# Attention with a gated mixture of experts on one core: where the second batch's sums are made, and the bank of a pair's sixth product

## The chip, the cores and the metric

The kernel runs on one core of a Trainium2 chip. The metric is the device time of one launch in microseconds. The runs shown are three; the profile is one further execution, with its own time.

## The reference

`x` has 2 batches of 2048 tokens of 512 features. Everything is float32. Cut to what matters:

```python
x = L0_attn_x
xn = layernorm(x)
# attention on xn
x_norm = layernorm(xn) * gamma + beta
q, k, v = x_norm @ qkv                     # 512 -> 3 x 512
scores = q @ k.T / sqrt(512)               # causal, per batch
out = softmax(scores) @ v
s = out @ o_proj + xn
# experts on xn: 8 experts, 2 chosen for a token, hidden 352
top_scores, top_idx = top_k(xn @ gate_w.T + gate_b + bias, 2)
comb = one_hot(top_idx) weighted by softmax(top_scores)
h = silu(xn @ w1 + b1)
y = (h @ w2 + b2) summed with comb
return x + s * silu(y)
```

## The kernel before

The kernel has three stages, and all of its work is put in an order written out by hand: every engine runs its instructions in the order in which the program emits them, so an instruction that waits holds back all that comes after it on the same engine, and the same is true of each engine's DMA queue. There is no planner.

1. Up to about 200 us: normalization, folding of weights, projections to queries, keys and values (stored in DRAM), and routing.
2. Up to about 610 us: the experts, 68 slots of 128 tokens, with results in `y_d` in DRAM.
3. From there: attention, with the gate and the output. The change lies here.

Attention works on tiles of 128 queries. There are 32 tiles, `NT`, and the loop `for s in range(NT + OUT + 2)` (L1409) takes one per step. The list `seq` (L810) says which: steps 0 to 15 are the tiles 15 to 0 of the first batch, and steps 16 to 31 are tiles 8, 9, 0, 1, 6, 7, 2, 3, 4, 5, 10, 11, 12, 13, 14, 15 of the second. Keys and values come in blocks of 512 tokens, `NBB` = 4 to a batch. `K` is 4, the first block of the second batch.

A step `s` emits, in this order:

- every second step, the loads of the next pair's queries (`fetch_q`, on the SP queue);
- `attended` (L1348) for a tile three or four steps back: ACT scales and shifts the product with values, DVE adds the residual; and `emit`, which is on POOL (multiply by the gate, add `x`) and stores the output;
- the scores of tile `s` on PE, in chunks of up to 512 keys (`chunk_scores`, L989), each in a PSUM bank of pool `ps_a`; DVE masks the diagonal and takes maxima. Between the chunks DVE runs `join_p` (L1168), which puts together the probabilities of tile `s-1` that a DMA has transposed;
- `end_scores` (L1080: the negated maximum `nm`), `divisor` (L1312), `exponentials` (L1131): ACT writes the probabilities, POOL splits them into 16-bit halves (`pu`), an SP DMA transposes them (`puT`). A tile of up to 384 keys is turned by PE instead (`turn_p`, L1161: transposes into a bank of `ps_a`, and a copy on ACT);
- up to four loads of the second batch's keys and values (`fetch_parts`, SP queue; the list `parts_b` gives the step from which each is due), and some sums on DVE, of which below;
- the product with values of tile `s-2` (`values`, L1175; a bank of `ps_b`), or the pieces of the fast form;
- every second step `gate` (L1338): four DVE operations on two rows of the experts' results, then a Silu on ACT; and `gather_y`, POOL's indirect loads of such rows.

The pairs in `FAST` (L959), which are steps 0 to 7 and 26 to 31, take a fast form with seven products in place of eight. `fast_scores` (L1029) does it for scores against the first two blocks, `values_first`, `values_next` and `values_end` (L1257 to L1310) for the product with values. These need sums made ahead on DVE:

- `query_sums` (L1007, tile `sq`, one buffer): four operations on the pair's queries, made in the odd step before;
- `block_sums` (L1018, tile `tk`, one buffer): four operations on two blocks of keys, once for each batch;
- `combine_v` (L1201, tile `vT`, three buffers): four operations on one block of values; each of the fast form's three blocks has its own.

In `fast_scores` each of the seven products (`made`) takes a bank from the list `pools` in turn, and DVE adds the products to the scores in SBUF. The first one is copied out by ACT (L1065). The sixth is the one with `q[:, 3]` and `b22` (in the profile `p<-k,sq`), the seventh the one with `a22` and `k[:, 3]` (`p<-tk,q`, in its second appearance). `ps_a` has five banks, `ps_b` three (L1092 and L1093).

Before, the second batch's sums are placed by these lines at the end of the step's work on scores:

```python
combine = {20: K, 22: K + 1, 26: K + 2}
...
            if s in combine:
                combine_v(combine[s])
            if 21 <= s < 25:
                block_sums(K, (s - 20,))
            if s % 2 and s > 3 and s // 2 + 1 in FAST:
                query_sums(s + 1, nc.vector)
```

Of the kernel before, what the change touches and what calls it, by code (L numbers as in the profile page):

```python
# [26 lines left out]
def gated_attention_moe(  # L27
# [27 lines left out]
    nc = tc.nc  # L55
# [7 lines left out]
    NBB = S // TB  # L63
# [895 lines left out]
    FAST = (0, 1, 2, 3, 13, 14, 15)  # L959
# [5 lines left out]
    def begin_scores(s):  # L965
        b, t, first = place(s)
        widths[s] = [TB] * (b - first) + [(t + 1) * P]
        mx = sm.tile([P, NBB], F32, name=f"mx_{s}", tag="mx")
        nm = sm.tile([P, 1], F32, name=f"nm_{s}", tag="nm")
        scored[s] = mx, nm, []  # L970
# [36 lines left out]
    def query_sums(s, engine):  # L1007

        q = qsums[s] = sq.tile([P, 4, ND // 2, P], F32, name=f"sq_{s}", tag="sq")
        (a11, a12), (a21, a22) = (  # L1010
            [aqs[seq[s] // 2][:, d, ts(seq[s + i] % 2, P)] for d in kds] for i in range(2)
        )
        engine.tensor_tensor(q[:, 0], a21, a22, ALU.add)
        engine.tensor_tensor(q[:, 1], q[:, 0], a11, ALU.subtract)
        engine.tensor_tensor(q[:, 2], a11, a21, ALU.subtract)
        engine.tensor_tensor(q[:, 3], a12, q[:, 1], ALU.subtract)

    def block_sums(first, parts=(1, 2, 3, 4)):  # L1018

        if 1 in parts:  # L1020
            bsums[first] = kt.tile([P, 4, ND // 2, TB], F32, name=f"tk_{first}", tag="tk")
        k = bsums[first]
        (b11, b12), (b21, b22) = ([aks[first + j][:, d, :] for j in range(2)] for d in kds)
        for i, x1, x2 in (1, b12, b11), (2, b22, k[:, 0]), (3, b22, b12), (4, b21, k[:, 1]):
            if i in parts:
                engine = nc.gpsimd if i == 3 and first == 0 else nc.vector
                engine.tensor_tensor(k[:, i - 1], x1, x2, ALU.subtract)
# [64 lines left out]
    ps_b = psum(att, name="ps_b", bufs=3)  # L1092
    ps_a = psum(att, name="ps_a", bufs=5)  # L1093
# [13 lines left out]
    for i in range(NS):  # L1107
        experts_step(i)
        if i >= 8 and i % 2 == 0 and early:
            f, b, c = early.pop(0)  # L1110
# [90 lines left out]
    def combine_v(b, parts=(1, 2, 3, 4), engine=nc.vector):  # L1201

        v = avs[b].rearrange("p (i h) d -> p i h d", h=2)
        if b not in avts:
            avts[b] = cp.tile([P, 2, 4, D // 2], F32, name=f"vT_{b}", tag="vT", bufs=NBB - 1)
        t1, t2, t3, t4 = (avts[b][:, :, i, :] for i in range(4))
        b11, b12, b21, b22 = (v[:, :, h, c] for h in range(2) for c in (LO, HI))
        for i, dst, x1, x2 in (1, t1, b12, b11), (2, t2, b22, t1), (3, t3, b22, b12), (4, t4, b21, t2):
            if i in parts:
                engine.tensor_tensor(dst, x1, x2, ALU.subtract)  # L1210
# [115 lines left out]
    def gather_y(s):  # L1326

        rows[s] = [op.tile([P, 2, D], F32, name=f"yg0_{s}", tag="yg0")]
        for i in range(2):
            rows[s].append(op.tile([P, D], F32, name=f"yg1_{s + i}", tag="yg1"))  # L1330
            n = seq[s + i]
            for k, y in enumerate((rows[s][0][:, i, :], rows[s][-1])):
                nc.gpsimd.indirect_dma_start(  # L1333
                    out=y, out_offset=None, in_=y_d,
                    in_offset=bass.IndirectOffsetOnAxis(ap=posi[k][:, n : n + 1], axis=0),
                )
# [57 lines left out]
    K = NBB  # L1394
# [3 lines left out]
    parts_b = [(s, f, b, c) for s, f, b in parts_b for c in range(ND)]  # L1398
    parts_b.sort(key=lambda part: part[0])

    combine = {20: K, 22: K + 1, 26: K + 2}

    def fetch_parts(s, most):
        while parts_b and most and parts_b[0][0] <= s:
# [4 lines left out]
    for s in range(NT + OUT + 2):  # L1409
        fast = s // 2 - 1 in FAST  # L1410
        pair = (s, s + 1) if s // 2 in FAST else (s,)
        if s < NT and (s % 2 == 0 or len(pair) == 1):
            for k in pair:
                if s:
                    begin_scores(k)
                room(k)
        n = s // 2 + 1
        if s % 2 == 0 and NQ <= n < NT // 2:
            for c in range(2):
                fetch_q(n, c)  # L1420
        if s == 0:
            fetch_parts(s, NBB * ND)
            block_sums(0)
        late = []
        for k in range(NT):
            if k not in AHEAD:
                wait = 4 - k % 2 if k // 2 in FAST else 3
                if s == k + wait:
                    late.append((attended, k))
                if s == k + wait + 1:  # L1430
                    emit(k)
        if len(pair) == 1 or s % 2:
            for f, *args in late:
                f(*args)
        for k in range(NT):
            if s == (NT - 1 if k in AHEAD else k + 2 - k % 2 if k // 2 in FAST else k + 1):
                fetch_inputs(k)
        if s == NT - 1:
            gather_y(NT - 2)
        joins = []  # L1440
        for k in () if s == 1 else (0, 1) if s == 2 else (s - 1,):
            if 0 <= k < NT - 1 and not by_te(k):
                joins += [(join_p, k)] * len(halves[k])
        chunks = []
        if s < NT and s != 1:
            chunks = [(k, j) for k in ((1,) if s == 0 else (s,)) for j in direct(k)]
        if s == 0:

            for k, j in chunks:
                chunk_scores(k, j)  # L1450
            chunks = []
        if s < NT and s % 2 == 0 and len(pair) == 2:
            pools = [(ps_b, "b")] * (NBB - 1) + [(ps_a, "a")] if s < 3 else [(ps_a, "a")]
            if s == 2:
                joins = [(combine_v, b, (1,)) for b in range(NBB - 1)] + joins
            now = 5 if s == 2 else 1
            fast_scores(s, pools, late + joins[:now])
            joins = joins[now:]
            if s == 0:
                query_sums(2, nc.gpsimd)  # L1460
        for k, j in chunks:
            chunk_scores(k, j)
            if s != 3 and joins:
                f, *args = joins.pop(0)
                f(*args)
        if s != 3:
            for f, *args in joins:
                f(*args)
        if 0 <= s - 1 < NT and by_te(s - 1):

            values(s - 2)
            turn_p(s - 1)
        if s < NT and s != 1:
            end_scores(s)
        if fast and s % 2 == 0 and 2 < s < NT:
            combine_p(s - 2)
        if 0 <= s - 1 < NT:
            divisor(s - 1)
        if s < NT:
            if s != 1:  # L1480
                exponentials(s)
            if s % 2 == 0 and len(pair) == 2:
                maximum(s + 1, turned[s + 1][:, : 2 * TB], 0)
            if s == 0:
                end_scores(1)
                exponentials(1)
            fetch_parts(s, 4)
            if s in combine:
                combine_v(combine[s])
            if 21 <= s < 25:  # L1490

                block_sums(K, (s - 20,))
            if s % 2 and s > 3 and s // 2 + 1 in FAST:
                query_sums(s + 1, nc.vector)
        if s == 2:
            pass
        elif s == 3:
            combine_p(0, (1, 3, 2))
            for b in range(NBB - 1):
                combine_v(b, (2,))  # L1500
            values_first(0)
            combine_p(0, (4,))
            for b in range(NBB - 1):
                combine_v(b, (4,))
            values_next(0)
            for f, *args in joins:
                f(*args)
            values_end(0, [lambda: query_sums(s + 1, nc.vector)])
        elif fast and s % 2 == 0:
            values_first(s - 2)  # L1510

            if s != NT - 2:
                values_next(s - 2)
        elif fast and s == NT - 1:
            values_next(s - 3)
            gate(s - 1)
            values_end(
                s - 3, [lambda: join_p(s)] * len(halves[s]) + [lambda: combine_p(s - 1)]
            )
            for k in AHEAD:  # L1520
                make_ahead(k)
        elif fast:
            values_end(s - 3)
        elif 0 <= s - 2 < NT and not (s - 1 < NT and by_te(s - 1)):
            values(s - 2)

        for k in range(0, NT - 2, 2):
            if s == (k + 2 if k + 2 in AHEAD else k + 3):
                gate(k)
        for k in range(0, NT - 2, 2):  # L1530
            if s == k + 1:
                gather_y(k)
        if s == 1:
            for b in range(NBB - 1):
                combine_v(b, (3,), nc.gpsimd)
# [45 lines left out]
```

## Time and profile before

| | |
|---|---|
| median of 3 runs | 1059.25 us |
| lowest, highest | 1057.97, 1065.2 us |
| profiled execution | 1057.82 us |
| its span | 1056.1 us |
| PE busy | 1038.8 us (98%) |
| DVE busy | 644.1 us (61%) |
| POOL busy | 432.4 us (41%) |
| ACT busy | 312.6 us (30%) |

The span runs from the first to the last instruction; the rest of the execution's time lies around it. PE is TensorE, PEld its weight loads, DVE VectorE, ACT ScalarE, POOL GpSimd, SP the engine that issues most DMAs. A float32 matmul shows as two entries of PE, so a product over two chunks of 128 is "x4". The end of a matmul is modelled and overlaps the next start, so distances are better taken from start to start. In a line of the timeline, the brackets hold the time for which the engine was idle just before and the engine and line that ended it. Steps 10 to 13 of attention lie at 773 to 812 us of this profile, steps 20 to 27 at some 858 to 941 us (by PE's scores).

### The profile page before, as it was taken

The page shows a single profiled execution, that of the slowest core. Times are in us where ns is not written, and L with a number is a line of the kernel's source. Part 1 is how long each engine was busy: PE and PEld are TensorE (multiplying, and loading weights), DVE is VectorE, ACT ScalarE, POOL GpSimd, SP SyncE. Part 2 cuts the span into 40 slices and gives each one's busy share as a digit, 9 for nine tenths or more (in the row PEclk, how much of TensorE's full clock was granted, in tenths as well). Part 3 has the DMA queues.
Part 4 walks back from the last instruction along what each step waited for, and adds up shares of the span by engine and source line. Part 5 has one row for each costly group of instructions (what it writes and reads, how often), then busy time and mean ns, then how long its engine had stood idle before and what let it go on. Part 6 is the DMA issues. An engine that isn't in the chain of part 4 may idle for free.

```text
span 1056.1 us, 12196 instructions
## 1 busy us (share of the span) xinstructions
PE 1038.8 (98%) x3554; PEld 616.2 (58%) x3554; DVE 644.1 (61%) x1227; ACT 312.6 (30%) x643; POOL 432.4 (41%) x469
## 2 busy tenths in 40 slices
PE   8999999999999999999999999999999999899998
PEld 3687886444555555555545446676665544447577
DVE  4797884775333333334335459767655668688686
ACT  3222221211322322322355322122334443422330
POOL 2364250003433333334332127354547776754372
PEclk9999999999999999999999999999999999999999
DMA  8699989946999999999897257445668768744361
GB/s 302 180 283 282 282 263 339 340 142 171 221 221 227 222 233 228 223 232 218 207 187 159 58 191 180 118 101 139 184 169 270 214 202 231 185 112 120 96 156 40
DMA packets 300512, 209.33 MB, mean 198 GB/s; under 512 B 234520, under 2 KB 247576, under 8 KB 299424
## 3 DMA queue, kind: packets, MB, share of 16 engines
q1 hardware_dynamic: 281248, 146.12, 55.5%
q0 software_dynamic: 10560, 35.17, 13.0%
q10 hardware_dynamic: 8640, 27.27, 7.1%
q8 instruction: 30, 0.49, 0.2%
q14 instruction: 34, 0.28, 0.1%
HBM read 92.89 MB, written 60.03 MB: 145 GB/s over the span
## 4 chain that ended last, share of the span: by engine, by line
PE 77%; POOL 6%; issue 6%; DVE 5%; DMA 3%; ACT 2%; SPq 0%; ACTq 0%; POOLq 0%; DVEq 0%
PE py L921 16%; PE ph L882 15%; PE p L1236 9%; PE ps L994 8%; PE p L400 7%; PE p L1046 6%; PE pj L341 3%; PE pw L207 3%; PE po L1188 3%; PE pj L346 3%; PE p L1188 2%; POOL yg L1333 2%; POOL pu L1148 1%; DMA zuT<-zu 1%; POOL o L1362 1%
## 5 line engine op out<-in xcount | busy, mean ns | idle before, releaser
L921 PE MATMUL py<-w,ht 128*128 (+3 forms) x408 | 187.1, 594 | 0.0
L882 PE MATMUL ph<-w,xT 128*128 (+1 forms) x544 | 173.2, 460 | 0.7 <-POOL keep L1103 0.7
L929 DVE COPY y<-py 128x512 f32<-128x512 f32 x68 | 46.9, 690 | 179.0 <-PE py L921 172.9
L994 PE MATMUL ps<-k,q 128*128 128x512 f32 (+3 forms) x416 | 143.0, 495 | 0.0
L882 PEld LDWEIGHTS ph<-w,xT 128*128 128x128 f32 (+1 forms) x544 | 97.5, 181 | 73.1 <-issue 34.5
L907 ACT ACTIVATE ht<-ht,b1sel 128x128 f32<-128x128 f32 (+3 forms) x237 | 73.1, 375 | 224.1 <-DVE ht L901 224.1
L892 POOL COPY hu<-h 128x704 uint16<-128x704 uint16 x68 | 52.4, 771 | 204.1 <-ACT h L890 124.7
L1148 POOL COPY pu<-pT 128x1024 uint16<-128x1024 uint16 (+2 forms) x74 | 84.0, 1167 | 126.3 <-ACT pT L1138 67.3
L921 PEld LDWEIGHTS py<-w,ht 128*128 128x128 f32 (+3 forms) x408 | 73.4, 182 | 75.4 <-issue 37.4
L994 PEld LDWEIGHTS ps<-k,q 128*128 128x128 f32 x416 | 74.6, 190 | 67.6 <-issue 57.7
L768 POOL DMA_INDIRECT xs<-zu_d,toki x68 | 68.9, 1014 | 69.3 <-DVE toki L642 57.9
L1188 PE MATMUL po<-v,pT 128*128 128x512 f32 x182 | 81.2, 593 | 1.2 <-DVE pT L1170 1.2
L1333 POOL DMA_INDIRECT yg<-y_d,posi x64 | 64.2, 1003 | 36.5 <-DVE yg L1344 22.1
L264 POOL COPY zu<-z 128x1024 uint16<-128x1024 uint16 x32 | 35.2, 1100 | 78.0 <-DVE z L249 78.0
L1170 DVE COPY pT<-puT 128x1024 uint16<-128x1024 uint16 (+2 forms) x74 | 55.9, 787 | 7.4 <-DMA puT<-pu 7.4
L1188 PEld LDWEIGHTS po<-v,pT 128*128 128x128 f32 x182 | 34.0, 190 | 40.0 <-issue 37.8
L413 DVE TENSOR_TENSOR so<-p,so 128x512 f32<-128x512 f32 x70 | 45.8, 686 | 16.5 <-DMA v_d<-so 9.3
L1354 DVE SCALAR_TENSOR_TENSOR o<-xo,xscale,o 128x512 f32<-128x512 f32 x30 | 28.7, 962 | 41.9 <-ACT o L1351 17.3
L842 DVE COPY xT<-xhT 128x1024 uint16<-128x1024 uint16 x68 | 47.2, 693 | 10.6 <-PE ph L882 5.7
L1052 DVE TENSOR_TENSOR pT<-p,pT 128x512 f32<-128x512 f32 x49 | 32.8, 687 | 25.5 <-PE p L1046 13.8
L1362 POOL TENSOR_TENSOR o<-o,yg 128x512 f32<-128x512 f32 x30 | 41.8, 1393 | 13.5 <-DVE o L1354 12.5
L1138 ACT ACTIVATE pT<-ps,nm 128x512 f32<-128x512 f32 (+3 forms) x52 | 30.0, 581 | 56.6 <-DVE nm L1082 37.3
(246 smaller groups left out, 1670.5 us busy)
## 6 DMA issues: line engine op xcount, KB each, us to landing
y_d<-y SPq DMA_DIRECT2D x68, 256.0 KB
zu_d<-zu SPq DMA_DIRECT2D x32, 264.0 KB
x<-in_x_dram SPq DMA_DIRECT2D x32, 256.0 KB
kt_d<-kT ACTq DMA_DIRECT2D x8, 1024.0 KB
k<-kt_d SPq DMA_DIRECT2D x32, 256.0 KB
q<-qt_d SPq DMA_DIRECT2D x32, 256.0 KB
v<-v_d SPq DMA_DIRECT2D x32, 256.0 KB
xo<-in_x_dram SPq DMA_DIRECT2D x32, 256.0 KB
```

The lines of the kernel that those rows point to most:

```text
L400: nc.tensor.matmul(ps[:, r, :], lhsT=lhs[:, c, ts(r, P)], rhs=rhs[:, c, :], start=(c == 0), stop=(c == 1),)
L768: nc.gpsimd.indirect_dma_start(out=xs, out_offset=None, in_=zu_d, in_offset=bass.IndirectOffsetOnAxis(ap=toki[:, i : i + 1], axis=0),)
L882: nc.tensor.matmul(ph[at, :], lhsT=xT[:, c, at], rhs=rhs[k], start=(c == 0), stop=(c == ND - 1),)
L907: nc.scalar.activation(ht[:hn, c, at], ht[:hn, c, at], AF.Silu, bias=b1sel[:hn, c, j : j + 1])
L921: nc.tensor.matmul(py[at, :], lhsT=ht[:k, c, at], rhs=rhs[n], start=(c == 0), stop=(c == NH - 1),)
L994: nc.tensor.matmul(ps[:, :w], lhsT=aqs[seq[s] // 2][:, c, ts(t % 2, P)], rhs=aks[first + j][:, c, :w], start=(c == 0), stop=(c == ND - 1),)
L1046: nc.tensor.matmul(ps, lhsT=x[:, c], rhs=y[:, c], start=(c == 0), stop=(c == ND // 2 - 1))
L1148: nc.gpsimd.tensor_copy(pu[:, : 2 * w].rearrange("p (h d) -> p h d", h=2), turned[s][:, k : k + w].bitcast(U16).rearrange("p (d h) -> p h ...
L1170: nc.vector.tensor_copy(turned[s][:, k : k + w].bitcast(U16).rearrange("p (i t h) -> p i t h", t=P, h=2), puT[:, : 2 * w // P, :].rearrang ...
L1188: nc.tensor.matmul(dst, lhsT=turned[s][:, ts(k, P)], rhs=avs[first + k // BT][:, k % BT, cols], start=(start and k == k0), stop=(k == k1 - 1),
L1236: nc.tensor.matmul(dst, lhsT=a[:, k], rhs=v(k), start=(k == 0), stop=(stop and k == n - 1))
L1333: nc.gpsimd.indirect_dma_start(out=y, out_offset=None, in_=y_d, in_offset=bass.IndirectOffsetOnAxis(ap=posi[k][:, n : n + 1], axis=0),)
```

## The change

It has four parts, all in attention.

- The sums of values of the second batch, before in steps 20, 22 and 26 with four operations each, are made with two operations in each of steps 10 and 11 (block K+2) and of 12 and 13 (block K+1), and one in each of steps 24 to 27 (block K).
- The sums of keys, one operation in each of steps 21 to 24, are made in steps 20 to 23.
- The query sums of steps 5, 25, 27 and 29 are emitted before the step's scores instead of after them.
- In `fast_scores`, from step 4 on, the sixth of the seven products takes a bank of `ps_b`, and the seventh the next one of `ps_a`; before, all seven took banks of `ps_a`. (The list for steps 0 and 2 is written anew and is the same.)

```diff
-    combine = {20: K, 22: K + 1, 26: K + 2}
+    later = {}
+    for steps, f, b in (
+        ((10, 10, 11, 11), combine_v, K + 2), ((12, 12, 13, 13), combine_v, K + 1),
+        ((20, 21, 22, 23), block_sums, K), ((24, 25, 26, 27), combine_v, K),
+    ):
+        for i, step in enumerate(steps):
+            later.setdefault(step, []).append((f, b, (i + 1,)))
...
         if s == NT - 1:
             gather_y(NT - 2)
+        if s % 2 and s > 3 and s // 2 + 1 in FAST:
+            query_sums(s + 1, nc.vector)
         joins = []
...
         if s < NT and s % 2 == 0 and len(pair) == 2:
-            pools = [(ps_b, "b")] * (NBB - 1) + [(ps_a, "a")] if s < 3 else [(ps_a, "a")]
+            pools = [(ps_a, "a")] * 5 + [(ps_b, "b"), (ps_a, "a")]
+            if s < 3:
+                pools = [(ps_b, "b")] * 3 + [(ps_a, "a")]
...
             fetch_parts(s, 4)
-            if s in combine:
-                combine_v(combine[s])
-            if 21 <= s < 25:
-
-                block_sums(K, (s - 20,))
-            if s % 2 and s > 3 and s // 2 + 1 in FAST:
-                query_sums(s + 1, nc.vector)
+            for f, *args in later.pop(s, []):
+                f(*args)
```

## The prediction

> **What bounds the kernel now.** I read the page's engine line first, then PE's waits, then busy time by stretch, and last the timelines of PE, DVE and ACT around each PE gap. TensorE is busy 98% of the span:
>
> ```profile
> PE 1038.8 (98%) x3554; PEld 616.2 (58%) x3554; DVE 644.1 (61%) x1227; ACT 312.6 (30%) x643; POOL 432.4 (41%) x469
> ```
>
> The span is 1056.1 us, so all of PE's gaps come to 17.3 us, and the change adds and removes no matmul. Removing every gap would gain 1.6%; the change can only reach those of the attention stage. PE's waits there (from 600 us on) are
>
> ```profile
> PE p L1046 <- ACT yg L1346: 1.7, 1, 1.7
> PE p L1046 <- DVE sq L1014: 1.3, 1, 1.3
> PE po L1188 <- DVE pT L1170: 1.2, 1, 1.2
> PE py L921 <- DVE w2c L869: 0.9, 1, 0.9
> PE p L1236 <- DVE u L1253: 0.6, 1, 0.6
> PE p L1046 <- ACT pT L1065: 0.4, 1, 0.4
> ```
>
> Columns: total us, times, longest. Three of these six lie at sums of keys, queries and banks: L1046 is a product of fast_scores. The w2c wait belongs to the experts. Where DVE is fullest is seen by stretch (PE, PEld, DVE, ACT, POOL busy):
>
> ```profile
> 745.00:790.00 45.00, 45.00 (x153) 28.03 (x152) 25.61 (x53) 15.02 (x24) 21.27 (x21) 1.00 0.64 171
> 870.00:910.00 40.00, 38.77 (x105) 18.72 (x105) 31.45 (x49) 14.43 (x23) 26.52 (x23) 1.00 0.76 215
> 910.00:950.00 40.00, 36.99 (x88) 16.04 (x86) 31.79 (x54) 12.91 (x21) 24.78 (x21) 1.00 0.56 133
> ```
>
> DVE has 57% in the first and 79% in the last two, and PE loses time only there. Step 26 in PE's timeline:
>
> ```profile
> 910.30 3.60 PE L1046 MATMUL p<-k,q 128*128 128x512 f32 x8
> 915.19 5.39 PE L1046 MATMUL p<-tk,sq 128*128 128x512 f32 x12 [1.30 <-DVE sq L1014]
> 922.29 1.98 PE L1046 MATMUL p<-k,sq 128*128 128x512 f32 x4 [1.71 <-ACT yg L1346]
> 924.11 1.88 PE L1046 MATMUL p<-tk,q 128*128 128x512 f32 x4
> ```
>
> Products 1 and 2, then 3 to 5, then 6, then 7. The idle in brackets is counted from a modelled end, so I use starts instead. In step 30, which has no stall, product 1 starts at 981.17 and product 6 at 989.75: 8.58 us. Here it is 922.29 - 910.30 = 11.99, a loss of **3.41 us**. In step 28 it is 950.45 - 941.28 = 9.17, a loss of **0.59**.
>
> ACT shows why product 6 waited. With five banks it takes the bank of product 1, which is free only after ACT has copied it, and ACT is in order behind the gate's Silu:
>
> ```profile
> 919.41 1.28 ACT L1346 ACT_TABLE_LOAD   x1 [4.16 <-DVE yg L1344]
> 920.71 1.06 ACT L1346 ACTIVATE yg<-yg 128x1024 f32<-128x1024 f32 x1
> 921.67 0.57 ACT L1065 COPY pT<-p 128x512 f32<-128x512 f32 x1
> ```
>
> **What the Trainium skill says.** "Perfetto Trace Analysis", section Matmuls: independent matmul groups should rotate through different PSUM banks, so that ACT or DVE evacuates one beside the next. Product 6 is the opposite case, and the trace agrees: 1.71 us shown idle. "SBUF — State Buffer", section Who interferes with whom: a DVE operation with two SBUF inputs contends with a GpSimd operation that reads SBUF, by an exclusive lock. The trace agrees: a sum of values is 0.68 us by itself (at 865.91) and 1.52 beside POOL's copies (at 933.93). "ScalarE: Activation LUTs", section What ACT_TABLE_LOAD costs, gives some 1.28 us for the load plus a drain of some 1.38; the trace has 1.28 and the Silu straight behind it, so 1.28 is used.
>
> **The change, part by part.**
>
> Sixth product in a values' bank (steps 4, 6, 26, 28, 30). It no longer waits for product 1's copy. Product 7 does now, as it takes that bank: it is wanted one product, 1.72 us, later. The values' pool has three banks; in step 26 the oldest is that of the values of step 21, which ACT read at 902.4. The values allocated after it go one bank further round; their previous contents are read long before in each case (the nearest, attended of step 24's values at 950.29, against a second use at some 963). So no new wait: nothing. The bank alone would let product 7 start at 922.3 instead of 924.11, so it is worth 1.8 us in step 26 even if ACT doesn't move, and the 0.59 of step 28.
>
> Query sums first (steps 5, 25, 27, 29). Four operations of 0.42 us (1.7 at best; 2.73 in step 25, beside POOL). Product 3 waited for the second of them, at 914.62. The queries' DMA was issued at 899.21, so it has landed. In front, they are behind attended of step 22 and ahead of the maxima and joins of step 25: some 1.7 us later for these. What is queued behind on DVE is a join that waited 2.13 us for its DMA in any case (DVE at 912.36), so this hides it. In steps 5 and 29 DVE was idle 4.32 and 4.38 us there, waiting for PE: nothing. In step 27 the join after it waits for its transposed copy (landing 939.08): nothing.
>
> Key sums one step earlier (20 to 23). Four of 1.21 us. In step 20 it lies in the wait in which the four sums of K's values now lie (865.91 to 868.5, then DVE idles 1.00 until ACT's output): both directions cost nothing, so step 21 gets part 2 for part 1 and does not move. The wait of values(21) at 887.53, where PE lost 887.53 - 882.70 - 3.43 = 1.40 us, comes before step 22's sums and therefore **stays**.
>
> Sums of values taken out of steps 20, 22 and 26. Step 22: 889.29 to 892.57 goes, 3.28 us, with DVE not idle until 900.1. So step 23's gate, ACT's Silu and step 24's attended come some 3.2 us sooner. Step 24 has a sum of 0.7 for a key sum of 1.31, some 0.6 more. In step 25 the query sums have left the place before the gate, against one sum of values of 0.7. The gate of step 25 ends some 5 us sooner than 919.3, and the copy of product 1, which ended at 922.24, is done at about 917, before product 6 is wanted (918.9). So all 3.41 us of step 26 go. In step 26 931.88 to 936.6 shrinks to one sum, and in step 27 the copy of product 1 comes early enough: the 0.59 goes as well. Gain: 3.41 + 0.59 = **4.00 us**.
>
> Sums of values put into steps 10 to 13. The values of K+2 are issued at 736.08 and those of K+1 at 789.05 to 791.0, needed at some 804: landed. The sums' three buffers were last read in step 9. Two sums a step, 0.68 each with overlap, 1.35 us. Step 10: DVE idles 783.4 to 786.44: hidden. Step 11: straight before the gate (792.15), so Silu and step 12's attended, nm and transposes are 1.35 later. Step 12: DVE idles 803.4 to 806.0: hidden. Step 13: again before the gate (810.52): 1.35 more, 2.7 in all. And there the cover ends:
>
> ```profile
> 814.35 1.06 ACT L1346 ACTIVATE yg<-yg 128x1024 f32<-128x1024 f32 x1
> 815.32 0.76 ACT L1351 ACTIVATE o<-po,xshift,ri 128x512 f32<-128x512 f32 x1
> 816.67 0.48 ACT L1166 COPY pT<-pt 128x384 f32<-128x384 f32 x1 [0.60 <-PE pt L1165]
> ```
>
> The copy is of the probabilities turned by PE; PE uses them in values(13), whose weight loads begin at 817.21, and the copy ends at 817.15. ACT had 0.60 us of slack ahead of it, so 2.7 - 0.6 = **2.1 us** of new wait. Bounds: 0 if the two steps' own waits (xo at 806, the join at 809.58) absorb the first 1.35 and half the rest; 3 if POOL's copies double one step's sums. I take 2.05. What is late next: banks for scores(17), with about 0.5 us to spare by the same sums. In step 16 PE has three chunks, 7.9 us, and ACT is released by PE's transposes at 829.7, so DVE's lag ends there.
>
> **Sum.** -4.00 + 2.05 = -1.95 us on a profiled execution of 1057.82 (span 1056.1 and 1.7 around it): 1055.9. The median of the runs shown is 1.43 above that execution, which gives 1057.3. I take the middle, **1056.6 us**.
>
> **Rivals.**
> - *Cover holds*: the waits of steps 12 and 13 absorb the sums, no stall at 817. For it: DVE idles there. Against it: these waits are ends of a chain through ACT and POOL that starts with DVE itself. Gain 4.0, or 5.4 if the wait of values(21) goes too: 1054.6, down to 1053.
> - *Lag carried (the slower side)*: steps 11 and 13 delay the ring of gate, Silu, attended and maxima, and the delay survives step 16. Then values(13) loses up to 3 us, a bank of scores(17) 0.5 and values(21) 1 more; against it only the 2.4 that the banks win by themselves. That is +2.1, about 1060.7. It decides once the new waits pass 4.0. Against it: PE's long step 16.
> - *Not what it says*: product 7, which inherits product 1's bank, waits as product 6 did, and the query sums wait for their DMA: nothing gained, 2.05 lost or hidden, 1058.6 to 1060. Against it: the arithmetic of 1.72 us, and the landing.
> - *A large loss* of over 1%: a head-of-line wait on DVE for a load or a buffer. Nothing in the trace shows one.
>
> **How the numbers follow.** Forecast 0.55, cover holds 0.22, lag carried 0.13, not what it says 0.06, large loss 0.04. The range runs from the gain of all four waits less a microsecond of spread between runs to the slower rival with the same: **1052.5 to 1063 us**. About 1% (10.6 us) is what a measurement of this kernel tells from no change. No case of gain reaches it, since it is most of all PE's gaps: faster 0.02, within 1% 0.94, slower 0.04.
>
> **What would show it.** Right: product 6 starts 8.6 us after product 1 in steps 26 and 28; values(13) waits some 2 us for ACT's copy, near 817; values(21) still waits for a join; the sum of values has 2 operations in each of steps 10 to 13. Wrong: a bracket at product 7, no wait near 817, or a wait of a DVE sum for a load in steps 10 to 13.

## The result, and the profile after

The changed kernel takes 1056.25 us (median; 1053.07 to 1058.56), the kernel before, run beside it, 1059.39 us (1057.15 to 1065.2). The ratio is 0.9968 with a 95% interval of 0.9957 to 0.9978. So it is faster by 0.3%, and the forecast of 1056.6 us came near it; below it will be seen that the total fits better than its terms.

The page's engine line after:

```profile
PE 1038.5 (99%) x3554; PEld 616.4 (59%) x3554; DVE 649.6 (62%) x1227; ACT 312.0 (30%) x643; POOL 432.9 (41%) x469
```

As many matmuls as before in a span of 1052.1 us: what is gained is gaps. DVE is busy 5.5 us longer, though it runs the same 1227 instructions. PE's waits after 600 us:

```profile
PE po L1188 <- DVE pT L1170: 1.2, 1, 1.2
PE po L1188 <- ACT pT L1166: 1.1, 1, 1.1
...
PE p L1046 <- issue: 0.4, 1, 0.4
```

The three of L1046 in before, 1.7, 1.3 and 0.4, are gone. The values' wait for DVE (1.2, in values(21)) has stayed, and there are two new rows: 1.1 for ACT's copy of turned probabilities, and 0.4 at a product of step 26. (values(21) is the product with values for the tile of step 21; it is emitted two steps later, behind the scores of step 23.) Busy time in the three stretches of before:

```profile
745.00:790.00 45.00, 45.00 (x151) 27.79 (x150) 27.32 (x57) 15.03 (x24) 21.41 (x20) 1.00 0.62 169
870.00:910.00 40.00, 38.83 (x105) 18.76 (x104) 28.90 (x45) 14.33 (x23) 27.57 (x24) 1.00 0.80 219
910.00:950.00 40.00, 39.56 (x95) 17.73 (x94) 32.92 (x56) 14.78 (x23) 23.53 (x20) 1.00 0.54 129
```

DVE has 1.7 us more in the first, 2.6 less in the second, and 1.1 *more* in the third, where PE nevertheless has 2.6 us more work done. The product that lost most before, step 26 in PE's timeline:

```profile
910.53 3.60 PE L1046 MATMUL p<-k,q 128*128 128x512 f32 x8
913.96 5.31 PE L1046 MATMUL p<-tk,sq 128*128 128x512 f32 x12
919.11 1.88 PE L1046 MATMUL p<-k,sq 128*128 128x512 f32 x4
921.42 1.98 PE L1046 MATMUL p<-tk,q 128*128 128x512 f32 x4 [0.44 <-issue]
```

Product 6 starts 919.11 - 910.53 = 8.58 us after product 1, the distance without a stall. Product 7 starts 10.89 after it, where 10.30 is the distance without a stall, so 0.59 us remain. ("issue" in the bracket means that the profile names nothing that was waited for.)

**How much of the difference is the change's?** The profiled spans differ by 4.0 us. I split each trace at the start of step 0's product 1 (PE, first line of L1046) and at the same product of steps 26, 28 and 30:

| | starts at | to 26 | 26 to 28 | 28 to 30 | 0 to 30 |
|---|---|---|---|---|---|
| before | 616.60 | 293.70 | 30.98 | 39.89 | 364.57 |
| after | 615.51 | 295.02 | 28.17 | 39.20 | 362.39 |
| difference | -1.09 | +1.32 | -2.81 | -0.69 | **-2.18** |

1.1 us of the 4.0 lie ahead of attention, which the change doesn't touch, and 0.8 after step 30, at a product that waits for DVE's `u` (L1253) in step 31: 0.6 shown idle in before, none here, 0.8 in another execution of the same kernel. So in these two traces the change itself is worth -2.18 us, and this distance serves below for comparing kernels. It comes from one execution of each kernel, but it repeats well: up to step 26, before, the bank alone and the query sums alone have 293.70, 293.68 and 293.66, and two executions of the changed kernel have 295.02. The timed runs say somewhat more, 2.3 to 4.6 us by the interval of the ratio, and 1.2 to 3.9 in a second series further down.

### The profile page after: what moved, and what is told of

The parts are those of the page before. It is cut to its first block, busy times and chain, and to the rows that moved or that the text cites. A ratio compares the mean times of both kernels' runs of the same rounds, so it can differ in the third digit from the quotient of the medians.

```text
span 1052.1 us, 12198 instructions
## 1 busy us (share of the span) xinstructions
PE 1038.5 (99%) x3554; PEld 616.4 (59%) x3554; DVE 649.6 (62%) x1227; ACT 312.0 (30%) x643; POOL 432.9 (41%) x469
## 4 chain that ended last, share of the span: by engine, by line
PE 80%; issue 5%; POOL 4%; DMA 4%; DVE 3%; ACT 2%; SPq 2%; ACTq 0%; POOLq 0%; DVEq 0%
PE py L921 16%; PE ph L882 15%; PE p L1236 11%; PE ps L994 9%; PE p L1046 8%; PE p L400 5%; PE pj L341 3%; PE po L1188 3%; PE pw L207 3%; PE pj L346 3%; PE p L1188 2%; DMA zuT<-zu 1%; SPq L271 1%; POOL yg L1333 1%; DMA puT<-pu 1%
```

## The experiments

The kernels below differ from before or after by the edit shown; those with a ratio were also timed beside before.

### The bank alone, the sums alone, the query sums alone

My theory: the bank and the lighter DVE each do a part. Rivals: the bank is only a cushion and DVE's moves make the gain; or, the other way round, the moved sums do little without the bank.

The bank alone, on before:

```diff
-            pools = [(ps_b, "b")] * (NBB - 1) + [(ps_a, "a")] if s < 3 else [(ps_a, "a")]
+            pools = [(ps_a, "a")] * 5 + [(ps_b, "b"), (ps_a, "a")]
+            if s < 3:
+                pools = [(ps_b, "b")] * 3 + [(ps_a, "a")]
```

> The kernel before with the sixth product's bank alone. My theory (the gain comes from both the bank and DVE's lighter steps 22 to 26): product 3 of step 26 still waits for the query sums (1.3 us shown), product 6 no longer waits, product 7 waits until product 1's copy; product 1 to product 7 in step 26 takes about 12.0 us in place of 13.81, in step 28 10.3 in place of 10.88; values(13) has no wait. Gain 2.4 us. Rival (the bank is only a cushion and DVE's moves make the gain): step 26 keeps 13.3 us or more, gain under 1 us.

Measured: 362.82 us from step 0 to 30, so -1.75; ratio 0.9983 (0.9966 to 1.0). Step 26 in PE's timeline:

```profile
910.56 3.60 PE L1046 MATMUL p<-k,q 128*128 128x512 f32 x8
915.45 5.39 PE L1046 MATMUL p<-tk,sq 128*128 128x512 f32 x12 [1.29 <-DVE sq L1014]
...
922.54 1.98 PE L1046 MATMUL p<-tk,q 128*128 128x512 f32 x4
```

Product 3 still waits for the query sums, and product 6 (at 920.67) follows with hardly a stall. Product 7 starts 11.98 after product 1 against 13.81 in before: 1.83 gained, as reckoned. In step 28 next to nothing is gained, which is why the gain stays below the 2.4 expected: product 7 starts 10.88 after product 1, in before 10.99, because it inherits both the bank and the wait for its copy.

The moved sums alone, without the bank, the query sums at their old place (after, with the lines below):

```diff
-        if s % 2 and s > 3 and s // 2 + 1 in FAST:
-            query_sums(s + 1, nc.vector)
         joins = []
...
-            pools = [(ps_a, "a")] * 5 + [(ps_b, "b"), (ps_a, "a")]
-            if s < 3:
-                pools = [(ps_b, "b")] * 3 + [(ps_a, "a")]
+            pools = [(ps_b, "b")] * (NBB - 1) + [(ps_a, "a")] if s < 3 else [(ps_a, "a")]
...
             for f, *args in later.pop(s, []):
                 f(*args)
+            if s % 2 and s > 3 and s // 2 + 1 in FAST:
+                query_sums(s + 1, nc.vector)
```

> The sums of values and of keys moved as in the changed kernel; the query sums last in their step and all seven products in the five banks, as before. My theory now: without POOL's emit beside the query sums the gate of step 25 ends some 3 us sooner than before, so products 1 to 7 of step 26 take 10.3 to 10.9 us and of step 28 10.3; values(13) waits 1.1 to 1.3 us. Net gain 2.4 to 2.8 us. Rival (the bank is needed): product 6 still waits over 1 us in step 26, products 1 to 7 take over 11.8, and the net gain is under 1.5 us.

Measured: 364.52, which is -0.05; ratio 0.9987 (0.997 to 1.0004). Up to step 26 it loses 1.25 us (294.95), from there on it gains 1.30. My theory of this run falls, and the rival has it: of step 26's products,

```profile
915.84 3.60 PE L1046 MATMUL p<-k,q 128*128 128x512 f32 x8
...
926.93 1.98 PE L1046 MATMUL p<-k,sq 128*128 128x512 f32 x4 [0.87 <-ACT pT L1065]
```

and the joins of steps 24 and 25 in DVE's timeline:

```profile
908.78 1.63 DVE L1170 COPY pT<-puT 128x1024 uint16<-128x1024 uint16 x1 [1.96 <-DMA puT<-pu]
916.54 0.69 DVE L1170 COPY pT<-puT 128x1024 uint16<-128x1024 uint16 x1 [2.01 <-DMA puT<-pu]
```

Product 6 starts 11.09 us after product 1, and so loses 11.09 - 8.58 = 2.5 us where before lost 3.41: freeing 3 us of DVE brought it 0.9. The joins tell why. They wait 1.96 and 2.01 us for transposed probabilities, so DVE comes early to a transfer that does not: the one for step 24's join is issued 12.58 us ahead of product 1 here and 12.42 in before.

The query sums first, alone (on before, with the two lines of `query_sums` moved ahead of `joins = []`):

```diff
+        if s % 2 and s > 3 and s // 2 + 1 in FAST:
+            query_sums(s + 1, nc.vector)
         joins = []
...
-            if s % 2 and s > 3 and s // 2 + 1 in FAST:
-                query_sums(s + 1, nc.vector)
```

> The query sums first in their step and nothing else changed. My theory now: in steps 25 and 27 they run beside POOL's emit and take some 3.5 and 5.2 us in place of 2.7 and 1.6, so the gate is no earlier; product 3's wait in step 26 goes (1.3 us) but product 6's grows by as much, products 1 to 7 take 13.8 or more there, and in step 28 10.9 to 13. Loss of 0 to 3 us. Rival (as predicted: hidden behind the join's wait for its DMA): product 3's wait goes and product 6's does not grow, gain 1.3 us.

Measured: 364.43, -0.14; ratio 0.999 (0.9978 to 1.0002). Step 26:

```profile
914.75 1.88 PE L1046 MATMUL p<-tk,sq 128*128 128x512 f32 x4
917.32 3.70 PE L1046 MATMUL p<-tk,sq 128*128 128x512 f32 x8 [0.70 <-ACT pT L1138]
923.03 1.98 PE L1046 MATMUL p<-k,sq 128*128 128x512 f32 x4 [2.01 <-ACT pT L1065]
```

Product 3, the first line, starts at once now, 3.44 us after product 1. What it wins is lost again at product 4 (0.70, for step 25's exponentials) and at product 6 (2.01, for the copy of product 1): an earlier stall for the most part only moved to a later one. The expected loss of up to 3 us did not come, and neither did the rival's gain of 1.3.

So -1.75, -0.05 and -0.14 add up to -1.94 of the -2.18, and of this net gain the bank makes most. But the -0.05 of the moved sums is a gain of 1.30 less a loss of 1.25 in other steps. Counted from step 26 to 30 alone, the three give 1.73, 1.30 and 0.10 of the changed kernel's 3.50. The intervals of all three ratios reach 1 or pass it, so these parts rest on the traces. Together the three make somewhat more than their sum. No two of them were run together, so it isn't shown which pair does.

### The new wait at values(13)

values(13) is the product with values for step 13's tile, emitted behind the scores of step 15. Theory: the sums of steps 11 and 13, which lie ahead of the gate, make its wait. Steps 10 and 12 have no gate and idle time, so all of them go there (after, with):

```diff
-        ((10, 10, 11, 11), combine_v, K + 2), ((12, 12, 13, 13), combine_v, K + 1),
+        ((10, 10, 10, 10), combine_v, K + 2), ((12, 12, 12, 12), combine_v, K + 1),
```

> The changed kernel, with all four sums of K+2 in step 10 and all four of K+1 in step 12, none in 11 and 13. My theory (the two sums ahead of the gate in steps 11 and 13 delay Silu, attended and the copy of the turned probabilities): DVE idles some 3 us in steps 10 and 12, so the sums are hidden, the wait of values(13) of 1.11 us goes, and the time is some 1.2 us below the changed kernel. Rival (the wait is made by the longer work of DVE in steps 10 to 13 as such, wherever it stands): the wait stays at 0.8 to 1.3 us or goes to another product.

Measured: 361.10, 1.29 less than after; ratio 0.997 (0.9958 to 0.9981). Its PE timeline from the scores of step 15 to values(13):

```profile
815.43 1.06 PE L994 MATMUL ps<-k,q 128*128 128x128 f32 x8
816.37 2.84 PE L1188 MATMUL po<-v,pT 128*128 128x512 f32 x6
```

and values(13) in after, where those scores start at 815.34:

```profile
817.50 2.84 PE L1188 MATMUL po<-v,pT 128*128 128x512 f32 x6 [1.11 <-ACT pT L1166]
```

From the scores to the values it is 0.94 us here and 2.16 in after (0.89 in before). The wait came from where the sums were put, and four of them in step 10 and in step 12, which have no gate, cost nothing.

### The wait of values(21)

Theory: it stays after the change because the key sum of step 21 lies ahead of that step's gate. On the kernel just shown, the second key sum goes to step 20:

```diff
-        ((20, 21, 22, 23), block_sums, K),
+        ((20, 20, 22, 23), block_sums, K),
```

> The kernel with the sums of values in steps 10 and 12, and parts 1 and 2 of the key sums both in step 20, none in 21. My theory: the wait of values(21) (1.15 us shown, 1.34 by starts) is DVE's lag in step 22, which starts at the gate of step 21; a key sum of 1.21 us stands just before that gate, while DVE idles after step 20's sum. Without it the gate, Silu, attended and the joins of step 22 come 1.2 us sooner and the wait falls to 0 to 0.3 us. Rival (the joins wait for their DMA or for ACT's exponentials): the wait stays at 1.0 or more. Nothing else moves.

Measured: 359.86, another -1.24; to step 26 it is -1.35. Ratio 0.9958 (0.9943 to 0.9974). Values(21) in after, whose scores start at 882.99, and in this kernel with its scores:

```profile
887.76 7.11 PE L1188 MATMUL po<-v,pT 128*128 128x512 f32 x16 [1.17 <-DVE pT L1170]
```

```profile
886.37 3.60 PE L994 MATMUL ps<-k,q 128*128 128x512 f32 x8
889.80 7.03 PE L1188 MATMUL po<-v,pT 128*128 128x512 f32 x16
```

3.43 us, the time of the scores, in place of 4.77. The theory holds.

### A values' bank for product 7 too

Theory: the 0.59 us left at product 7 are the copy of product 1 (ACT's L1065), whose bank it takes. With values' banks for both, it goes. On the kernel with sums in steps 10 and 12:

```diff
-            pools = [(ps_a, "a")] * 5 + [(ps_b, "b"), (ps_a, "a")]
+            pools = [(ps_a, "a")] * 5 + [(ps_b, "b"), (ps_b, "b")]
```

> The kernel with the sums of values in steps 10 and 12, and the seventh product too in a bank of the values. My theory: product 7 of step 26 waits 0.6 us by starts for the copy of product 1, whose bank it takes; with another bank product 1 to product 7 takes 10.30 in place of 10.90, and the next chunk of scores, which takes product 1's bank now, starts 1.7 us later than that and does not wait. Gain 0.6 us. Rival: the values' three banks run short, and the values' product of step 24, which now takes the bank read by attended in step 26, waits on PE for 0.5 us or more.

Measured: 360.83, -0.27; ratio 0.9968 (0.9954 to 0.9982). In step 26 product 7 starts 10.30 after product 1, no stall left, and 26 to 28 takes 27.47 instead of 28.17. But 28 to 30 takes 39.63 instead of 39.20: 0.43 of the 0.70 is given back, at a new wait for DVE's `s`.

```profile
959.72 2.42 PE L1236 MATMUL p<-vT,s 128*128 128x256 f32 x10 [0.16 <-DVE s L1230]
```

The bracket has 0.16, but this product starts 0.32 later after product 1 of step 28 than without the second bank (21.41 against 21.09), and the next one 0.42 later. That is all of it.

### Everything in idle places

All sums only in even steps, which have no gate, with values' banks for products 6 and 7 (on the kernel with sums in steps 10 and 12):

```diff
-        ((20, 21, 22, 23), block_sums, K), ((24, 25, 26, 27), combine_v, K),
+        ((16, 16, 20, 20), block_sums, K), ((24, 24, 26, 26), combine_v, K),
```

> All together: values' sums of K+2 in step 10, of K+1 in step 12, of K two each in steps 24 and 26, key sums two each in steps 16 and 20, query sums first, products 6 and 7 in values' banks. My theory: no wait of PE is left in attention but that of step 31 for POOL's last rows (0 to 0.7 us by run). From the first product of step 0 to the last matmul: 433.5 before, 430.6 in the changed kernel, 428.2 to 429 here; time some 2 us below the changed kernel, ratio to before 0.994 to 0.996. Rival (the waits are PE's own queue or DMA and not sums): 430 or more.

Measured: 431.93 us from step 0's product 1 to the end, where after has 432.49 and my theory was 428.2 to 429: wrong. From step 0 to 30 it is 361.02; ratio 0.9969 (0.9955 to 0.9982). PE's timeline has two new waits:

```profile
853.91 8.82 PE L1188 MATMUL po<-v,pT 128*128 128x512 f32 x20 [0.96 <-DVE pT L1170]
962.53 2.43 PE L1236 MATMUL p<-vT,s 128*128 128x256 f32 x10 [0.73 <-DVE s L1230]
```

The first comes with the two key sums in step 16, 2.4 us: the next kernel, the only other one with sums there, has it too (0.98), and in none of the rest does PE wait there for DVE. So the rival's number came, but not its reason: both waits are shown as waits for DVE. "No gate in this step" is not yet "idle".

### What sets the gate of step 25

In the prediction this gate ended some 5 us sooner; it ended 1.1 us sooner (9.04 us after product 1 of step 26 in before, 7.94 in after). Theory: DVE's work doesn't set it; the joins of steps 24 and 25 do. So on the kernel of the moved sums alone (no bank, query sums late), I leave steps 21 to 25 no sums of keys or values at all:

```diff
-        ((10, 10, 11, 11), combine_v, K + 2), ((12, 12, 13, 13), combine_v, K + 1),
-        ((20, 21, 22, 23), block_sums, K), ((24, 25, 26, 27), combine_v, K),
+        ((10, 10, 10, 10), combine_v, K + 2), ((12, 12, 12, 12), combine_v, K + 1),
+        ((16, 16, 18, 18), block_sums, K), ((20, 20, 20, 20), combine_v, K),
```

> Five banks and query sums last, as before, and no sum of keys or values on DVE in steps 21 to 25 (values' sums in 10, 12 and 20, key sums in 16 and 18). My theory now: DVE's lag at step 26 is set by the joins, which wait for transposed probabilities whose exponential stands on ACT behind the copy of a tile turned by PE; lighter DVE only waits longer for them. Product 3 still waits 1.0 us or more for the query sums and product 6 0.5 us or more. Rival (as predicted: DVE's load makes the lag): both waits go, products 1 to 7 of step 26 take 10.3 to 10.6 us.

Measured (one profile): the gate ends 7.77 us after product 1. DVE's timeline has the joins of steps 24 and 25 as

```profile
902.10 0.69 DVE L1170 COPY pT<-puT 128x1024 uint16<-128x1024 uint16 x1 [2.05 <-DMA puT<-pu]
910.50 0.70 DVE L1170 COPY pT<-puT 128x1024 uint16<-128x1024 uint16 x1 [3.77 <-DMA puT<-pu]
```

and product 6 still waits 1.71 us for ACT's Silu. With all these sums gone, DVE idles 5.8 us at two joins, and the gate is sooner by 1.3 us against before (the moved sums alone: 0.9). So far the theory holds: the joins set where DVE's work for this gate begins. They do not set all of it, as DVE runs from the second join to the gate's end without a pause, and 2.7 us of that are the query sums. In another part I was wrong: product 3's wait fell to 0.20 us, so the query sums, behind the second join, do follow DVE's load.

Why do the probabilities come no sooner? In step 23 ACT runs, in after,

```profile
895.28 0.48 ACT L1166 COPY pT<-pt 128x384 f32<-128x384 f32 x1 [4.56 <-PE pt L1165]
895.66 0.69 ACT L1138 ACTIVATE pT<-ps,nm 128x512 f32<-128x512 f32 x1
```

The exponentials that step 24 joins stand on ACT behind a copy that waits 4.56 us for PE, since step 22's tile (384 keys) is turned by PE. Counted from product 1 of step 26 the copy starts at -15.25 in after and in before (895.05). So I let the DMA turn that tile (the kernel of the moved sums alone, and `by_te`, which holds for tiles up to 256 keys now):

```diff
-        return sum(widths[s]) <= 3 * P
+        return sum(widths[s]) <= 2 * P
```

> The kernel with the sums alone moved (five banks, query sums last), and PE turns only tiles of up to 256 keys, so that the tiles of 384 keys in steps 13 and 22 go through POOL and a transposing DMA. My theory: the exponential of step 23 no longer stands behind ACT's copy of the turned tile, DVE's wait for transposed probabilities in step 24 (1.96 us) falls below 0.7, and the gate of step 25 ends 1.5 us or more sooner against product 1 of step 26 (7.8 us after it with the sums alone); product 6 waits less than 0.3 us. Rival (the copy isn't what holds the exponential; the DMA's own 3 us or the maxima do): the wait stays at 1.5 or more and product 6 still waits 0.6 or more. Either way a new join of 384 keys stands in steps 14 and 23.

Measured (one profile):

```profile
913.64 1.23 DVE L1170 COPY pT<-puT 128x1024 uint16<-128x1024 uint16 x1 [0.17 <-issue]
922.12 0.69 DVE L1170 COPY pT<-puT 128x1024 uint16<-128x1024 uint16 x1 [1.79 <-DMA puT<-pu]
```

The join of step 24 waits 0.17 in place of 1.96. Part of this is as explained. The transfer for it, in the DMA queue of SP, with the sums alone moved and here:

```profile
903.26 1.23 SPq L1154 DMA_TRANSPOSE puT<-pu  x1
```

```profile
906.77 1.23 SPq L1154 DMA_TRANSPOSE puT<-pu  x1
```

It is issued 14.02 us ahead of product 1 of step 26 in place of 12.58, 1.44 sooner, so the copy had held it back. But DVE comes to this join later, too: it has a new join of 384 keys in step 23, which waits 1.42, and its attended of step 24 is 1.70 later against product 1. Either would have taken most of the wait, and the join itself starts no sooner (7.15 us ahead of product 1 here, 7.06 with the sums alone), so this run does not settle what the copy costs. The gate is none the sooner for it, 8.77 us after product 1: step 25's join waits 1.79, and in ACT's timeline a table load of 1.28 us, at 915.67, lies ahead of the exponentials, having waited 3.58 for DVE.

Product 6 still lost some: 932.54 - 920.79 = 11.75 against 8.58, of which 1.87 shown at product 3 and 0.89 at product 6. All in all this kernel is slower (371.89 from step 0 to 30), above all by a new wait of 5.88 us at values(13), whose tile of 384 keys the edit takes from PE as well. What sets the gate of step 25 beyond these joins stays open.

### The best pair, and the change once more

The sums in 10 and 12, two key sums in 20, and two values' banks together; and the changed kernel itself in the same series:

> Values' sums of K+2 in step 10 and of K+1 in step 12, parts 1 and 2 of the key sums both in step 20, products 6 and 7 in banks of the values, query sums first. My theory (the three edits act at three separate places of PE's chain and add up): no wait at values(13), at values(21) or at product 7; from product 1 of step 0 to the end of the last matmul some 430.1 us, against 435.43 before, 432.49 in the changed kernel and 430.71 with the first two edits alone; time 2 us below the changed kernel. Rival (the last gain comes back as a new wait of the values' product or of the last rows): 430.7 or more.

> The changed kernel unchanged, beside the previous one. My theory: the attention stage repeats within 0.3 us where no DMA decides (432.2 to 432.8, or 0.7 more with the wait for POOL's last rows in step 31), while the start of product 1 of step 0, which was 615.5 to 620.9 us in the profiles so far, varies by run with the first stage, which the change doesn't touch. Rival (the 1.1 us by which that start was earlier in the changed kernel's profile belongs to the change): the start is again 615.3 to 615.7.

Measured: the changed kernel has 362.40 (362.39 the first time), ratio 0.9976 (0.9963 to 0.9989), median 1056.25; its distance from step 0 to 30 repeats to 0.01 us although product 1 of step 0 starts 1.65 us later than the first time. The combination has 359.68, ratio 0.9958 (0.9943 to 0.9973), median 1054.41. That is -4.9 against before and -2.7 against the change. The intervals of the two ratios overlap; the distance within the trace does tell them apart. Against two key sums in 20 without the second bank (359.86) it is only -0.18: the rival, that the second bank's gain comes back as a new wait, has it. Of the 0.81 of step 26, 0.60 are given back at the wait for `s` (L1230), where the bracket shows 0.33.

## Why the prediction was right or wrong

The sum was -4.00 + 2.05 = -1.95 us. Measured in attention: -2.81 - 0.69 in steps 26 to 30 and +1.32 before them, -2.18. By its steps:

**Sixth product in a values' bank: right.** 1.8 us was worked out for it alone in step 26; 1.83 was measured. No values waited for a bank. "The 0.59 of step 28" was wrong for the bank alone (0.11 gained), since product 7 takes the bank that product 6 gave up. "Perfetto Trace Analysis", section Matmuls, asks for rotation through banks; this case adds that with seven products and five banks the wait goes to the next one in turn, and that its size falls by that one product's time.

**"The gate of step 25 ends some 5 us sooner": this step failed.** It was 1.1. The first term held: step 24's attended on DVE stands 10.38 us ahead of product 1 of step 26, before 7.06, so 3.3 sooner. But then:

```profile
900.15 0.75 DVE L1354 SCALAR_TENSOR_TENSOR o<-xo,xscale,o 128x512 f32<-128x512 f32 x1 [3.13 <-ACT o L1351]
...
903.53 1.58 DVE L1170 COPY pT<-puT 128x1024 uint16<-128x1024 uint16 x1 [2.02 <-DMA puT<-pu]
```

2.02 of the 3.3 end in the join, which in before had not waited at all (its transfer is issued 0.16 us sooner than in before, counted from product 1). I had counted the work taken away from DVE and not asked when the join's data lands. Then the query sums, now first in step 25, meet POOL's `emit`:

```profile
908.55 1.48 DVE L1013 TENSOR_TENSOR sq<-q 128x256 f32<-128x256 f32 x1
910.07 1.37 DVE L1014 TENSOR_TENSOR sq<-sq,q 128x256 f32<-128x256 f32 x1
```

3.6 us for the four (0.41 each for the other two) where 1.7 was reckoned at best and 2.7 was their time in the old place, and the gate's own four operations take 3.5 us there where they took 2.5 in before. The gate's end, and on ACT the copy of product 1:

```profile
917.72 0.75 DVE L1344 SCALAR_TENSOR_TENSOR yg<-yg,share,yg 128x512 f32<-128x512 f32 x1
```

```profile
920.81 0.57 ACT L1065 COPY pT<-p 128x512 f32<-128x512 f32 x1
```

So this copy ended at 921.38 and not at about 917. Product 7 starts straight behind it, and 0.59 us stayed. That product 7 of step 26 nevertheless starts 2.9 us sooner (10.89 after product 1 for 13.81) comes of two things. It is now product 7 and not product 6 that stands behind the copy, 1.8 us further on in PE's order: the bank's doing. And the copy comes 1.1 us sooner, as the gate does. The prediction had the waits of step 26 right, but of the 3.41 us it promised for step 26, 0.59 were left because DVE's lighter steps moved the gate by 1.1 us and not by 5.

**Step 28: right, by the whole change.** Product 7 there has no stall, and 28 to 30 is 0.69 shorter; 0.59 was predicted.

**The new wait at values(13): right mechanism, mis-sized.** Predicted 2.05 of bounds 0 to 3, measured 2.16 - 0.89 = 1.27 us. The first 1.35, of step 11, came out as 1.5, its two sums being 1.43 and 1.52 us beside POOL:

```profile
791.08 1.43 DVE L1210 TENSOR_TENSOR vT<-v 128x512 f32<-128x512 f32 x1
792.43 1.52 DVE L1210 TENSOR_TENSOR vT<-v,vT 128x512 f32<-128x512 f32 x1
```

But they took that place from the gate's first two operations, which ran free of it in turn (0.62 and 0.75 us for 1.17 and 1.41), and so did the joins of step 12 (1.02 us for two; 2.24 in before). After those joins 0.9 of the 1.5 were left. Step 13 added 1.2, so that its gate came 2.1 us late and not 2.7; ACT's slack of some 0.6 was as read, some 0.2 more were taken up on the way from ACT to PE, and the rest is PE's wait. The term that was too large is the lag carried from step 11 to step 13. It is the lower bound's reason ("the steps' own waits absorb") in half.

**values(21) stays: right** (887.76 - 882.99 - 3.43 = 1.34, before 1.40), and the key sum ahead of the gate as its cause is shown by moving it.

**The rivals.** *Cover holds* is out by the wait at 817. *Lag carried* is out: banks for scores(17) show no wait. *Not what it says* has a point, product 7 inheriting the wait, but with 0.59 and not 3.41.

The two errors, a gain of 3.50 for 4.00 and a loss of 1.32 for 2.05, nearly cancel; that the total came nearer than its terms is luck. So is part of the hit on the time itself: 1056.6 was the middle between two bases, one execution and three runs. Between the medians measured side by side lie 3.14 us, where the sum has 1.95.

## What to carry to other kernels

When a step on an engine is made lighter, look up the next wait of that engine for something it doesn't make itself: the lead lasts to there and no further. When a product is stopped by a bank, one bank from another pool may do as much as moving a lot of work elsewhere (here 1.73 us against 1.30); check which product takes the old bank next. And put filling work into steps where nothing stands behind it that PE will soon wait for: the same eight sums cost 1.3 us with four of them ahead of two gates, and nothing with all of them in the even steps between. That a step has no gate is not enough, as the two sums in step 16 show; look at the trace of that step.

## What the runs showed of the hardware

- A DVE sum of two SBUF tensors takes more than twice as long while POOL runs the two operations of `emit` or its copies: 128x512 1.43 and 1.52 us for 0.68, 128x256 1.37 and 1.48 for 0.41. "SBUF — State Buffer", section Who interferes with whom, names the contention for the port; these are its sizes here, read from what overlaps in time, as no run takes POOL's work away. What I had not expected is that this is a place in time more than a property of the operation: put other operations into the contended place, and those behind run faster, as the gate of step 11 did.
- Where attention starts differs from run to run, by up to 5.75 us: product 1 of step 0 stands at 615.51 and 617.16 in two executions of the changed kernel, and at 615.14 to 620.89 over all these kernels, whose first two stages are the same. A difference of 2 us is read from within the stage, not from the span.
